# Edge products of 64 rows in the two halves of TensorE, four steps at a time in two banks

## The chip, the cores and the metric

The kernel runs on one core of a Trainium2 chip. The metric is the device time of one execution in microseconds; before and after are compared by the medians of several runs. The profile is that of one execution, taken by the hardware profiler.

## What is computed

Two graph layers with layer norm and residual on 6250 nodes of 256 features and 100000 edges. Every layer takes, for every node, the maximum over its incoming edges. The edges come sorted by `dst`.

```
def layer0(x, src, dst):                       # sweep 0
    e = relu((x[dst] - x[src]) @ theta_w.T + theta_b + x[src] @ phi_w.T + phi_b)
    return segment_max(e, dst)                 # 0 for a node without edges
x = layernorm(x + layer0(x, src, dst))
hv = x @ W_in + b_in
for W, b in ((W_u0, b_u0), (W_u1, b_u1)):      # sweeps 1 and 2
    m = relu(concat([hv[src], he]) @ W + b)    # he: 64 features per edge
    hv = where(has_in, segment_max(m, dst) + hv, hv)
out = layernorm(x + relu(hv @ W_ro + b_ro))
```

In sweeps 1 and 2 the product of `he` (64 features) with the last 64 rows of `W` is made per edge; the rest, `hv @ W[:256]`, is made per node and gathered. These are the edge products of the title.

## The kernel before

The edges are laid out as 782 steps of 128 edges, in 14 blocks (56 steps each, the last 54): partition p holds consecutive edges of a block along its steps. A sweep (`sweep(r)`, r = 0, 1, 2) walks the steps s = 0 to 781. Everything is in the order in which it is written (a manual schedule): every engine has its own queue, executes it in that order, and waits on semaphores.

**Gathers.** `sources(s)` (L790) is one indirect DMA on GpSimd (POOL): 128 rows of `table[r]` into step s of a tile `run` of 8 steps; there are 4 such tiles. It is issued 16 steps ahead (`AHEAD`). Sweeps 1 and 2 issue their first 24 steps (`EARLY`) from the end of the sweep before, with clipped indices that leave out node tile 0, whose table rows come last; these 24 steps get the rows of tile 0 by a one-hot product. Sweep 0 makes the first two steps of its first 20 tiles from raw rows of `x` instead (`raw_turn` transposes four blocks on TensorE, L798, ScalarE copies them, L800, `raw_pair` multiplies, L806).

**Edge products.** `pair(i)` serves two steps 2i and 2i+1. The features of both lie one above the other in `hT` (rows 0 to 63 the first step, rows 64 to 127 the second), and `whe` is a block-diagonal matrix of 128 rows by 512 columns, half of it zero. One product (L825) gives both steps in one bank of PSUM (`hp`, tag `he`, 3 banks). `pair` is issued 4 steps ahead. For the first 12 pairs SyncE fetches a row of indices (`row`, L822), VectorE makes a one-hot from it (`own`, L824), and two more products (L829) add the rows of node tile 0. `row` and `own` have two buffers each.

**The chain on VectorE.** For every two steps, L1030 adds the gathered rows of both to the bank `hp`; then each step does L1043, `run[s] = max(min(run[s-1], lim), row)`, a running maximum along the steps, which starts anew where the node changes.

**What follows.** When a tile of 8 steps is done, SyncE writes it to DRAM (`S<-run`, L1051); the buffer is free for new gathers when that has landed. At a block's end, `over_lanes` transposes the last step (`lp`, tag `tp`), `scan` on VectorE carries the maximum across the lanes, `back` transposes it back (`cp`, tag `tp`). Per tile of 128 nodes, `node` gathers the ends from S (L870, POOL), joins them with the carried ones and makes the node's products and the next table (`turned` with tag `tp`, `times` with tag `pr`). These are tasks, put into a list per step by `at(slot, f)` and called at the end of that step in the order in which they were put in. Sweep 0 also counts edges per node with one-hots (`count`: `ol` L710, `hist` L721).

**PSUM** has 8 banks: 3 of tag `he`, 2 of `tp`, 2 of `pr`, 1 of `v`.

Of the kernel before, what the change touches and what calls it, by code (L numbers as in the profile page):

```python
# [8 lines left out]
F32 = mybir.dt.float32  # L9
BF16 = mybir.dt.bfloat16  # L10
I32 = mybir.dt.int32
AF = mybir.ActivationFunctionType
OP = mybir.AluOpType
# [4 lines left out]
P = 128  # L18
N = 6250
D = 256  # L20
DE = 64
E = 100000
NT = 49
K = 8
# [11 lines left out]
BLOCKS = [56] * 13 + [54]  # L36
NB = len(BLOCKS)
FS = sum(BLOCKS)
FE = P * FS
FIRST = [sum(BLOCKS[:b]) for b in range(NB)]  # L40
# [4 lines left out]
EARLY = 3 * K  # L45
RAW = 40
# [21 lines left out]
def raw(s):  # L68

    i = s // K * 2 + s % K  # L70
    return i if s % K < 2 and i < RAW else None
# [525 lines left out]
def in_order(ctx: ExitStack, tc: tile.TileContext, g):  # L597
# [8 lines left out]
    nc = tc.nc  # L606
# [3 lines left out]
    s_e, head, x, x_sb, wd, s_r = (g[n] for n in ("s_e", "head", "x", "x_sb", "wd", "s_r"))  # L610
    part = g["part"]
    ctx.enter_context(tc.manual_schedule())
    one = ctx.enter_context(tc.tile_pool(name="one", bufs=1))
    work = ctx.enter_context(tc.tile_pool(name="work", bufs=2))
    psum = ctx.enter_context(tc.tile_pool(name="psum", bufs=2, space=PSUM))
# [9 lines left out]
    new0 = one.tile([P, D], F32, name="new0")  # L625
# [26 lines left out]
    bro = line(g["b_ro"], "bro")  # L652
    whe = []
    for r, w in enumerate((g["w_u0"], g["w_u1"])):
        t = one.tile([P, 2, D], F32, name=f"whe{r}")
        nc.vector.memset(t, 0.0)
        for s in range(2):
            nc.scalar.dma_start(t[s * DE:(s + 1) * DE, s, :], w[D:, :])
        whe.append(t)


# [38 lines left out]
    half = (NG + 1) // 2  # L700
    low = []
    for i in range(2):
        low.append(psum.tile([P, 512], F32, tag="he", name="low", bufs=3))
        n = min(half * K, FS - i * half * K)
        nc.scalar.copy(low[i][:, :n], lo[:, i * half * K:i * half * K + n])

# [18 lines left out]
    sums = []  # L725
# [29 lines left out]
        nc.vector.tensor_scalar(dest, a, mv[:, 0:1], sd, OP.subtract, OP.mult)  # L755

    def turned(a):
        tp = psum.tile([P, 512], F32, tag="tp", name="tp")
        for k in range(2):
            nc.tensor.transpose(tp[:, k * P:(k + 1) * P], a[:, k * P:(k + 1) * P], ident)  # L760
        aT = work.tile([P, 2, P], F32, name="aT")
        nc.scalar.copy(aT.rearrange("p k e -> p (k e)"), tp[:, :2 * P])  # L762
        return aT

    def times(aT, w, n, tag="pr"):
        ps = psum.tile([P, 512], F32, tag=tag, name="prod", bufs=3 if tag == "he" else 2)
        for k in range(2):
            nc.tensor.matmul(ps[:, :n], aT[:, k, :], w[:, k, :], start=(k == 0), stop=(k == 1))  # L768
        return ps

    def sweep(r):

        tasks = {}

        def at(slot, f, *a):
            tasks.setdefault(slot, []).append((f, a))
# [5 lines left out]
        runs = ahead.pop(r, {})  # L782
# [10 lines left out]

        def raw_turn(i):

            tp = psum.tile([P, 512], F32, tag="tp", name="tp")
            for q in range(4):
                nc.tensor.transpose(tp[:, q * P:(q + 1) * P], x_sb[:, 2 * i + q // 2, q % 2 * P:(q % 2 + 1) * P], ident)  # L798
            rT[i] = work.tile([P, K // 2, P], F32, tag="hT", name="rT", bufs=4)
            nc.scalar.copy(rT[i].rearrange("p k e -> p (k e)"), tp)  # L800

        def raw_pair(i):
            aT = rT.pop(i)
            hp[i * K // 2] = psum.tile([P, 512], F32, tag="pr", name="hp")
            for q in range(4):
                nc.tensor.matmul(hp[i * K // 2][:, q // 2 * D:(q // 2 + 1) * D], aT[:, q, :], wd[:, q % 2, :],  # L806
                                 start=q % 2 == 0, stop=q % 2 == 1)
# [5 lines left out]
            hT[c] = work.tile([P, K // 2, P], F32, name="hT", bufs=4)  # L813
            nc.scalar.dma_start(hT[c].rearrange("p q e -> p (q e)"), heT[c])

        def pair(i):
            c, q = divmod(i, K // 2)
            hp[i] = psum.tile([P, 512], F32, tag="he", name="hp", bufs=3)
            early = 2 * i < EARLY
            if early:  # L820
                row = work.tile([P, 2 * P], I32, name="row")
                nc.sync.dma_start(row, head[i:i + 1, :].to_broadcast([P, 2 * P]))  # L822
                own = work.tile([P, 2 * P], F32, name="own")
                nc.vector.tensor_scalar(own, row, part, None, OP.is_equal)  # L824
            nc.tensor.matmul(hp[i], hT[c][:, q, :], whe[r - 1].rearrange("p s f -> p (s f)"), start=True,  # L825
                             stop=not early)
            if early:
                for k in range(2):
                    nc.tensor.matmul(hp[i][:, k * D:(k + 1) * D], own[:, k * P:(k + 1) * P], new0, start=False, stop=k == 1)  # L829
            if q == K // 2 - 1:  # L830
                del hT[c]

        def over_lanes(b, last):

            lp = psum.tile([P, 512], F32, tag="tp", name="lp")
            nc.tensor.transpose(lp[:, 2 * P:3 * P], link[:, b:b + 1].to_broadcast([P, P]), ident)
            lim2 = work.tile([P, P], F32, name="lim2")
            nc.scalar.copy(lim2, lp[:, 2 * P:3 * P])
            for k in range(2):
                nc.tensor.transpose(lp[:, k * P:(k + 1) * P], last[:, k * P:(k + 1) * P], ident)  # L840
            to, of = cT[b % 2], cT[(b + 1) % 2]

            def scan():
                for k in range(2):
                    nc.vector.tensor_tensor_scan(to[:, k, 1:], lim2, lp[:, k * P:(k + 1) * P],
                                                 of[:, k, P:] if b else 0.0, OP.min, OP.max)
                if b:
                    nc.scalar.copy(to[:, :, 0:1], of[:, :, P:])
                else:
                    nc.vector.memset(to[:, :, 0:1], 0.0)  # L850

            def back():
                cp = psum.tile([P, 512], F32, tag="tp", name="cp")
                for k in range(2):
                    nc.tensor.transpose(cp[:, k * P:(k + 1) * P], to[:, k, :P], ident)
                carried_in.append(b)
                nc.scalar.copy(cs[:, b % KEPT, :D], cp[:, :D])

            at(FIRST[b] + BLOCKS[b], scan)
            at(FIRST[b] + BLOCKS[b] + 1, back)  # L860

        def node(t, g, b):

# [129 lines left out]
        b = 0  # L993
        for t in reversed(range(NT)):
            e = max(FIRST[SPAN[t][1]] + BLOCKS[SPAN[t][1]], begin)
            b = max(b + (gap if b < FS else 3), e + 4, min(e + AHEAD + 4, FS + 4))
# [11 lines left out]
        for s in range(-AHEAD if r == 0 else 0, FS):  # L1008
            if s + AHEAD < FS and (r == 0 or s + AHEAD >= EARLY):
                sources(s + AHEAD)  # L1010
            if r < 2 and s >= FS - FIRM:
                sources_next(s - (FS - FIRM))
            if s < 0:
                continue
            c, j = divmod(s, K)
            if r > 0:
                if s == 0:
                    for i in range(4):
                        features(i)
                    pair(0)  # L1020
                    pair(1)
                elif j == 0 and c + 3 < NG:
                    features(c + 3)
            if s % 2 == 0:
                two = runs[c][:, j:j + 2, :].rearrange("p s f -> p (s f)")
                if r > 0:
                    if s + 4 < FS:
                        pair(s // 2 + 2)
                    sums = hp.pop(s // 2)
                    nc.vector.tensor_add(sums, sums, two)  # L1030
                elif raw(s) is not None:
                    sums = hp.pop(s // 2)
                    i = raw(s) // 2
                    if i + 2 < RAW // 2:
                        raw_turn(i + 2)
                    if i + 1 < RAW // 2:
                        raw_pair(i + 1)
                else:
                    sums = two
            cur = runs[c][:, j, :]  # L1040
            row = sums[:, s % 2 * D:(s % 2 + 1) * D]
            if s > FIRST[blk]:
                nc.vector.scalar_tensor_tensor(cur, prev, lim[:, s:s + 1], row, OP.min, OP.max)  # L1043
            elif r > 0 or raw(s) is not None:
                nc.vector.tensor_copy(cur, row)
            prev = cur
            if j == K - 1 or s in (FS - 3, FS - 1):
                k = 2 if s == FS - 1 else j + 1
                to = S_w[P * FIRST[blk]:P * (FIRST[blk] + BLOCKS[blk]), :].rearrange("(p s) f -> p s f", p=P)
                at_ = s + 1 - k - FIRST[blk]  # L1050
                pending.append(nc.sync.dma_start(to[:, at_:at_ + k, :], runs[c][:, j + 1 - k:j + 1, :]))  # L1051
            if s == FIRST[blk] + BLOCKS[blk] - 1:
                over_lanes(blk, prev)
                blk += 1
            for f, a in tasks.pop(s, ()):
                f(*a)
# [62 lines left out]
```

## Time and profile before

| | |
|---|---|
| median of 7 runs | 3215.57 us (3211.86 to 3218.49) |
| profiled execution | 3214.67 us, span 3212.9 us |
| busy share of the span | PE 59%, DVE 66%, ACT 7%, POOL 75% |
| mean granted TensorE clock | 0.738 |
| first gather (L790) of sweep 0, 1, 2 | 61.8 us, 1091.6 us, 2143.4 us |

The profile names lines of the kernel (L825), engines (PE is TensorE, PEld its weight loads, DVE VectorE, ACT ScalarE, POOL GpSimd, SP SyncE) and tiles by their names in the program. A TensorE product of this type is recorded as two instructions.

### The profile page before, as it was taken

How to read it: one execution, taken by the hardware profiler on the slowest of the kernel's cores; microseconds unless marked ns; L12 is line 12 of the kernel's file. 1: busy time of each engine (PE TensorE's matmuls, PEld its weight loads, DVE VectorE, ACT ScalarE, POOL GpSimd, SP SyncE). 2: the span in 40 equal slices, each digit the busy share in tenths (PEclk: the TensorE clock that was granted, in tenths of full speed). 3: DMA queues.
4: the chain of work that ended last, by engine and by line, in shares of the span. 5: the costliest groups of instructions: out<-in, count | busy, mean ns of one | idle time of the engine just before them, and what ended most of it. 6: DMA issues, size and time to landing. Idle time of an engine off the chain costs nothing. (4 is left out here: it accounts for less than half of the span.)

```text
span 3212.9 us, 21650 instructions
## 1 busy us (share of the span) xinstructions
PE 1879.6 (59%) x4631; PEld 848.0 (26%) x4631; DVE 2127.8 (66%) x4750; ACT 238.7 (7%) x618; POOL 2394.8 (75%) x2500
## 2 busy tenths in 40 slices
PE   6663336566511266766666666657666666666665
PEld 5442222222200122322222222223332232222222
DVE  2788756555544376666666666657777777777766
ACT  2000001111100000000000000000001000000000
POOL 6767777777777767777777777776777777777775
PEclk8765557655655598788777877779888878887787
DMA  8769666656666676677767776767766676677775
GB/s 305 239 220 317 222 216 211 207 193 205 205 203 206 201 248 231 229 234 236 232 228 241 239 237 229 241 217 248 240 231 229 230 238 228 233 234 241 238 232 192
DMA packets 241821, 739.39 MB, mean 230 GB/s; under 512 B 52485, under 2 KB 95858, under 8 KB 204434
## 3 DMA queue, kind: packets, MB, share of 16 engines
q0 software_dynamic: 119664, 326.92, 34.2%
q1 hardware_dynamic: 69568, 337.85, 28.1%
q10 hardware_dynamic: 52450, 73.16, 6.9%
q8 instruction: 39, 0.64, 0.1%
q14 instruction: 100, 0.82, 0.1%
HBM read 404.56 MB, written 333.17 MB: 230 GB/s over the span
## 5 line engine op out<-in xcount | busy, mean ns | idle before, releaser
L790 POOL DMA_INDIRECT run<-table,s_s x2258 | 2165.6, 959 | 718.0 <-issue 606.2
L825 PE MATMUL hp<-whe,hT 128*128 128x512 f32 x1564 | 1055.2, 784 | 530.0 <-DVE run L1043 515.1
L1030 DVE TENSOR_TENSOR hp<-hp,run 128x512 f32<-128x512 f32 x782 | 543.9, 695 | 459.1 <-DMA run<-table,s_s 422.3
L1043 DVE SCALAR_TENSOR_TENSOR run<-run,lim,hp 128x256 f32<-128x256 f32 x1573 | 753.9, 479 | 46.8
L825 PEld LDWEIGHTS hp<-whe,hT 128*128 128x128 f32 x1564 | 326.5, 239 | 1077.0 <-DVE run L1043 1016.7
L1043 DVE SCALAR_TENSOR_TENSOR run<-run,lim 128x256 f32<-128x256 f32 x731 | 351.6, 481 | 233.3 <-DMA run<-table,s_s 220.7
L889 PE MATMUL v<-cs,pick 128*128 128x256 f32 (+1 forms) x438 | 167.4, 503 | 141.6 <-DVE pick L882 137.0
L768 PE MATMUL prod<-wcat,aT 128*128 128x512 f32 x196 | 174.4, 1041 | 23.2 <-ACT aT L762 23.2
L870 POOL DMA_INDIRECT m<-S,end_i x147 | 144.1, 981 | 52.6 <-issue 43.6
L889 PEld LDWEIGHTS v<-cs,pick 128*128 128x128 f32 x438 | 105.2, 260 | 253.9 <-issue 150.0
L721 PE MATMUL hist<-oh,ol 128*128 128x8 bf16 (+7 forms) x782 | 34.8, 167 | 177.7 <-DVE oh L716 177.7
L710 DVE TENSOR_TENSOR ol<-col,low 128x1024 bf16<-128x1024 bf16 x98 | 118.7, 1212 | 7.3 <-PE hist L721 7.3
L760 PE MATMUL tp<-ident,h_sb 128*128 128x128 f32 x196 | 49.1, 339 | 121.7 <-DVE h_sb L935 121.3
L932 ACT ACTIVATE m<-m,has 128x256 f32<-128x256 f32 x98 | 49.7, 508 | 692.4 <-DVE m L931 690.9
L760 PE MATMUL tp<-ident,x_sb 128*128 128x128 f32 x98 | 31.9, 426 | 113.6 <-DVE x_sb L755 85.7
L840 PE MATMUL lp<-ident,run 128*128 128x128 f32 x84 | 24.2, 383 | 124.1 <-DVE run L1043 116.4
L768 PE MATMUL prod<-wro,aT 128*128 128x256 f32 x196 | 79.1, 542 | 25.3 <-ACT aT L762 25.3
L721 PEld LDWEIGHTS <-ol 128*128 128x128 bf16 x782 | 36.3, 104 | 203.0 <-DVE ol L710 198.4
L768 PE MATMUL prod<-wt,xT 128*128 128x256 f32 x196 | 88.0, 596 | 0.4 <-DMA xT<-in_xTn 0.4
L762 ACT COPY aT<-tp 128x256 f32<-128x256 f32 x147 | 54.7, 372 | 449.4 <-PE tp L760 427.4
L768 PEld LDWEIGHTS prod<-wcat,aT 128*128 128x128 f32 x196 | 56.1, 314 | 89.1 <-issue 48.4
L760 PEld LDWEIGHTS tp<-ident,h_sb 128*128 128x128 f32 x196 | 23.9, 164 | 210.8 <-issue 122.5
(131 smaller groups left out, 1323.6 us busy)
## 6 DMA issues: line engine op xcount, KB each, us to landing
S<-run SPq DMA_DIRECT2D x291, 1024.0 KB, 4.8
hT<-in_heT ACTq DMA_DIRECT2D x196, 256.0 KB, 4.5
run<-table,s_s POOLq DMA_INDIRECT x2258, 3.4
table<-new ACTq DMA_DIRECT2D x98, 128.0 KB, 3.6
xg<-in_xTn SPq DMA_DIRECT2D x7, 896.0 KB, 9.5
xT<-in_xTn SPq DMA_DIRECT2D x49, 128.0 KB, 5.1
x_sb<-in_xn SPq DMA_DIRECT2D x7, 896.0 KB, 7.7
out<-new ACTq DMA_DIRECT2D x48, 128.0 KB, 2.5
```

Of the source, the lines that this page charges most:

```text
L710: nc.vector.tensor_tensor(ol[:, :k, :], col.unsqueeze(1).to_broadcast([P, k, P]), low[c // half][:, c % half * K:c % half * K + k].unsquee ...
L721: nc.tensor.matmul(hist[:, t0:t0 + w], ol[:, j, :], oh[:, j, :w], start=False, stop=(c == NG - 1 and j == k - 1))
L760: nc.tensor.transpose(tp[:, k * P:(k + 1) * P], a[:, k * P:(k + 1) * P], ident)
L762: nc.scalar.copy(aT.rearrange("p k e -> p (k e)"), tp[:, :2 * P])
L768: nc.tensor.matmul(ps[:, :n], aT[:, k, :], w[:, k, :], start=(k == 0), stop=(k == 1))
L790: nc.gpsimd.indirect_dma_start(out=runs[s // K][:, s % K, :], out_offset=None, in_=table[r][:SPARE + 1, :] if early else table[r], in_offs ...
L825: nc.tensor.matmul(hp[i], hT[c][:, q, :], whe[r - 1].rearrange("p s f -> p (s f)"), start=True, stop=not early)
L870: i = nc.gpsimd.indirect_dma_start(out=o["m"], out_offset=None, in_=S_r[:P * (FIRST[SPAN[t][1]] + BLOCKS[SPAN[t][1]]), :], in_offset=bass. ...
L889: nc.tensor.matmul(o["v"][:, :N1], p, cs[:, blk % KEPT, :N1], start=(blk == SPAN[t][0]), stop=(blk == SPAN[t][1]))
L932: nc.scalar.activation(o["m"], o["m"], AF.Relu, scale=has[:, t:t + 1])
L1030: nc.vector.tensor_add(sums, sums, two)
L1043: nc.vector.scalar_tensor_tensor(cur, prev, lim[:, s:s + 1], row, OP.min, OP.max)
```

## The change

`whe` becomes one matrix of 64 rows by 256 columns, held twice, in partitions 0 to 63 and in partitions 64 to 127; its two fills with zero go. `pair(i)` becomes `four(u)`, which serves steps 4u to 4u+3 in two banks. The first steps of the two pairs (4u, 4u+2) come out of rows 0 to 63 and go to the first bank, the second steps (4u+1, 4u+3) come out of rows 64 to 127 and go to the second. It is issued when step 4u-4 begins. VectorE adds the gathered rows of steps 4u and 4u+2 in one instruction at step 4u, and those of 4u+1 and 4u+3 at step 4u+1. The running maximum stays one instruction per step. In the first 24 steps the two one-hots of a four are made ahead of its products.

Tag `he` gets 4 banks, and tag `tp` 1 in place of 2. `scan` and `back` are put at the front of their step's task list.

```diff
     for r, w in enumerate((g["w_u0"], g["w_u1"])):
-        t = one.tile([P, 2, D], F32, name=f"whe{r}")
-        nc.vector.memset(t, 0.0)
+        t = one.tile([P, D], F32, name=f"whe{r}")
         for s in range(2):
-            nc.scalar.dma_start(t[s * DE:(s + 1) * DE, s, :], w[D:, :])
+            nc.scalar.dma_start(t[s * DE:(s + 1) * DE, :], w[D:, :])
...
-        tp = psum.tile([P, 512], F32, tag="tp", name="tp")
+        tp = psum.tile([P, 512], F32, tag="tp", name="tp", bufs=1)
...
-        ps = psum.tile([P, 512], F32, tag=tag, name="prod", bufs=3 if tag == "he" else 2)
+        ps = psum.tile([P, 512], F32, tag=tag, name="prod", bufs=4 if tag == "he" else 2)
...
-        def pair(i):
-            c, q = divmod(i, K // 2)
-            hp[i] = psum.tile([P, 512], F32, tag="he", name="hp", bufs=3)
-            early = 2 * i < EARLY
-            if early:
-                row = work.tile([P, 2 * P], I32, name="row")
-                nc.sync.dma_start(row, head[i:i + 1, :].to_broadcast([P, 2 * P]))
-                own = work.tile([P, 2 * P], F32, name="own")
-                nc.vector.tensor_scalar(own, row, part, None, OP.is_equal)
-            nc.tensor.matmul(hp[i], hT[c][:, q, :], whe[r - 1].rearrange("p s f -> p (s f)"), start=True,
-                             stop=not early)
-            if early:
+        def four(u):
+
+            c, q = divmod(u, K // 4)
+            hp[u] = [psum.tile([P, 512], F32, tag="he", name="hp", bufs=4) for _ in range(2)]
+            early = 4 * u < EARLY
+            n = min(2, FS // 2 - 2 * u)
+            for j in range(n):
+                i = 2 * u + j
+                if early:
+                    row = work.tile([P, 2 * P], I32, name="row")
+                    nc.sync.dma_start(row, head[i:i + 1, :].to_broadcast([P, 2 * P]))
+                    own = work.tile([P, 2 * P], F32, name="own")
+                    nc.vector.tensor_scalar(own, row, part, None, OP.is_equal)
                 for k in range(2):
-                    nc.tensor.matmul(hp[i][:, k * D:(k + 1) * D], own[:, k * P:(k + 1) * P], new0, start=False, stop=k == 1)
-            if q == K // 2 - 1:
+                    at_ = slice(k * DE, (k + 1) * DE)
+                    nc.tensor.matmul(hp[u][k][:, j * D:(j + 1) * D], hT[c][at_, 2 * q + j, :], whe[r - 1][at_, :],
+                                     start=True, stop=not early)
+                if early:
+                    for k in range(2):
+                        nc.tensor.matmul(hp[u][k][:, j * D:(j + 1) * D], own[:, k * P:(k + 1) * P], new0, start=False,
+                                         stop=True)
+            if q == K // 4 - 1:
                 del hT[c]
...
-            at(FIRST[b] + BLOCKS[b], scan)
-            at(FIRST[b] + BLOCKS[b] + 1, back)
+            for i, f in enumerate((scan, back)):
+                tasks.setdefault(FIRST[b] + BLOCKS[b] + i, []).insert(0, (f, ()))
...
-                    pair(0)
-                    pair(1)
+                    four(0)
...
-                if r > 0:
-                    if s + 4 < FS:
-                        pair(s // 2 + 2)
-                    sums = hp.pop(s // 2)
-                    nc.vector.tensor_add(sums, sums, two)
...
+            if r > 0:
+                if s % 4 == 0 and s + 4 < FS:
+                    four(s // 4 + 1)
+                if s % 4 < 2:
+                    n = min(2, (FS - s + 1) // 2)
+                    sums = hp[s // 4][s % 2].rearrange("p (a f) -> p a f", f=D)[:, :n, :]
+                    nc.vector.tensor_add(sums, sums, runs[c][:, j:j + 2 * n - 1:2, :])
+                row = hp[s // 4][s % 2][:, s % 4 // 2 * D:(s % 4 // 2 + 1) * D]
+                if s % 4 == 3:
+                    del hp[s // 4]
```

## The prediction, made before the changed kernel was run

> **What bounds the kernel now.** First the busy times and the waits of POOL: is an engine full, and what does it wait for?
>
> ```profile
> PE 1879.6 (59%) x4631; PEld 848.0 (26%) x4631; DVE 2127.8 (66%) x4750; ACT 238.7 (7%) x618; POOL 2394.8 (75%) x2500
> POOL run L790 <- issue: 620.2, 2032, 1.2
> POOL run L790 <- DVE run L1043: 43.6, 58, 7.5
> POOL m L870 <- issue: 43.6, 143, 0.3
> ```
>
> No engine looks full, but POOL is: a gather takes 0.95 us, and 0.30 us pass before the next with nothing awaited ("issue"), one per 1.25 us. The 2493 of L790, L870 and L76 at that pace are 3116 of the span's 3212.9 us. So what the end depends on is POOL's standing still beyond 0.30 us. I listed every such gap: 9.3 us in the prologue, 10.5 us in sweep 0 between 155 and 226 us (seven gaps), 11.8 us at the start of sweep 1, 7.8 us at that of sweep 2, 7.8 us before the last row gather. Nowhere else in 3000 us. The timeline of POOL, start of sweep 1:
>
> ```profile
> 1140.11 0.94 POOL L790 DMA_INDIRECT run<-table,s_s  x1 [7.45 <-DVE run L1043]
> 1141.35 0.95 POOL L790 DMA_INDIRECT run<-table,s_s  x1 [0.30 <-issue]
> ...
> 1153.93 0.95 POOL L790 DMA_INDIRECT run<-table,s_s  x1 [4.13 <-DVE run L1043]
> ...
> 1164.78 0.94 POOL L790 DMA_INDIRECT run<-table,s_s  x1 [1.15 <-DVE run L1043]
> ```
>
> There are four run tiles; POOL waits until VectorE has finished a tile and its `S<-run` has landed. After 1165 us VectorE is ahead for good: S of tile 2 leaves at 1159.39 us (step 23 done), and that moment alone fixes how late POOL is for the rest of the sweep. What VectorE does until then, from the timeline of all engines:
>
> ```profile
> 1119.99 2.08 PE L825 MATMUL hp<-whe,hT 128*128 128x512 f32 x2 [6.87 <-DMA hT<-in_heT]
> 1123.81 0.35 DVE L824 TENSOR_SCALAR own<-row,part 128x256 f32<-128x256 int32 x1 [9.54 <-PE hp L829]
> 1124.08 0.69 DVE L1030 TENSOR_TENSOR hp<-hp,run 128x512 f32<-128x512 f32 x1
> ...
> 1126.28 0.35 DVE L824 TENSOR_SCALAR own<-row,part 128x256 f32<-128x256 int32 x1 [0.53 <-PE hp L829]
> ...
> 1138.36 0.35 DVE L824 TENSOR_SCALAR own<-row,part 128x256 f32<-128x256 int32 x1 [6.28 <-DMA row<-in_head]
> ```
>
> Last the edge products, in the groups of instructions:
>
> ```profile
> L825 PE MATMUL hp<-whe,hT 128*128 128x512 f32 x1564 | 1055.2, 784 | 530.0 <-DVE run L1043 515.1
> L1030 DVE TENSOR_TENSOR hp<-hp,run 128x512 f32<-128x512 f32 x782 | 543.9, 695 | 459.1 <-DMA run<-table,s_s 422.3
> ```
>
> PE waits for VectorE, VectorE for gathers. Cheaper products gain nothing along the sweeps.
>
> **The change part by part.**
>
> *Products along the sweeps: 0.* Two pairs had 2 x 512 columns, a four has 4 x 256: the same columns if the halves run one after another, half if both run at once. L825 falls from 1055 us to between 530 and 1100 us. POOL's gathers hide it (gaps 0.30 us from 1165 to 2184 and 2213 to 3193 us). Cover gone: see the second rival. The Trainium skill (TensorEngine Tiling (Array Packing), section "Key Properties") says that such tiles load weights and multiply independently of each other, but also, against this change, that going from one tiling mode to another drains TensorE; nothing in this trace shows either, as all its products have the full height. By the first the sum below would stand at its low end, by the second at its high end.
>
> *VectorE along the sweeps: 0.* L1030 becomes 784 instructions of the same 512 elements (0.69 us). Step 4u now awaits gather 4u+2 in place of 4u+1, and after gather 4u+3 one add and three L1043 remain (0.69 + 3 x 0.51 = 2.2 us) in place of an add and two (1.7 us). It is 0.5 us later; a tile must be free only 24 gathers (30 us) after its last one was issued, of which landing (3.4), VectorE and S (5) take some 12. The two fills with zero (1.02 us at 51.6 us) stood where VectorE idled: 0.
>
> *Start of sweeps 1 and 2.* VectorE's queue now has `own` 0 to 3 ahead of the first add, not 0 to 2. `own` has two buffers, so `own` 3 waits until PE has read `own` 1. That moment is in the trace: 1126.28. The first add moves from 1124.08 to 1126.55; then add, copy, add and three L1043 (0.73 + 0.46 + 0.73 + 3 x 0.51 = 3.45, start to start in this stretch) end steps 0 to 3 at 1130.0, and steps 4 to 7 take 2 x 1.91 (before's pace per pair): 1133.8 against 1132.1. That is +1.7 us if the halves run one after another. At once, the two cold edge products (1.87 and 1.64 us) fall towards half, and nothing is left: 0. I take 1.2. Then `row` 6 and 7, on SyncE's queue behind `S<-run`, which waits for step 7: both are now needed before the add, and the second is issued 0.48 us after the first (1133.00, 1132.52): +0.3. `own` 9 needs the products with `own` 7, which ended 4.9 us after `own` 6 began (1143.3 - 1138.4), where VectorE is there after 4.6: +0 to 0.5. The third stage (`row` 10, 11) has the same +0.3, and its fours wait for PE instead: 0 to 0.7. Sum per sweep 0.6 to 3.5, I take 2.5, nearer to one after another, as the products of an early four alternate with full-height ones. Twice: **+5.0** (1.2 to 7.0). Each such us delays step 23, S, POOL and the end one to one.
>
> *One `tp` bank in sweep 0.* The start, from the timeline:
>
> ```profile
> 69.29 1.06 ACT L800 COPY rT<-tp 128x512 f32<-128x512 f32 x2
> 69.92 3.78 PE L806 MATMUL hp<-wd,rT 128*128 128x256 f32 x8 [14.24 <-ACT rT L800]
> ...
> 73.74 0.42 DVE L1045 COPY run<-hp 128x256 f32<-128x256 f32 x1 [20.97 <-PE hp L806]
> ```
>
> The second turn (four transposes, 0.6 to 1.1 us) was done long before; with one bank it follows the first copy and stands ahead of the first product: +0.9 (0.6 to 1.1). From there to 226 us VectorE never waits for a gather but for PE and back, and POOL waits for VectorE, so all of it arrives. At the ends of blocks 0 and 1, `lp` holds the bank until `scan`, and the next turn (130.29 before) waits for that (131.0): +0.7, and +0.6 at the second; PE's `hist` behind it holds VectorE's `ol` (idle 0.86 us there already). Bounds: 0 and 1.9 for both. Sum **+2.2** (0.6 to 3.0). Moving `scan` and `back` forward only changes places within a step: 0. The fourth `he` bank: 0, as `prod` in it is read a step later and made once in eight.
>
> *The tail.*
>
> ```profile
> 3194.86 0.70 DVE L1030 TENSOR_TENSOR hp<-hp,run 128x512 f32<-128x512 f32 x1 [3.21 <-DMA run<-table,s_s]
> ```
>
> From here before does two adds and four L1043: 3.4 us. After, gather 779 finds step 776 done at best: add, three L1043, then steps 780 and 781 with adds of 256 elements (0.42): 0.73 + 1.53 + 2 x 0.46 + 2 x 0.51 = 4.2. **+0.8** (-0.5 if gather 780 comes late, 2.0 if step 776 waits too). S, the last row gather and its chain follow one to one.
>
> Sum 5.0 + 2.2 + 0.8 = 8.0 (1.3 to 12.0). The profiled execution took 3214.67 us (span 3212.9 and 1.8 around it), 0.9 below the median of 3215.57. So 3222.7 by the profile and 3223.6 by the median; I say 3223. About 0.2% (6.4 us) is what a measurement can tell from no change.
>
> **Rivals.**
>
> *The halves run at once and the starts cost little: same.* For it: the two products of a pair of steps lie next to each other in PE's queue, in different rows and banks. Then the starts give 1 us, the sum is 1 to 6, and the time 3216 to 3221.
>
> *PE becomes the pace: far slower.* From 1170 to 2160 us PE is busy 642 of 990 us, 507 of them L825. If 64-row products took twice as long per column (loads not hidden, drains), PE would need 1149 us: 160 us more per sweep, some 3530 us. It decides from 855 us of edge products per sweep, 1.7 times now. Milder drains, at the 0.24 us that PE's loads sit idle for "issue" here, four in each of six early fours, add at most 5.8 us per sweep.
>
> *Faster: POOL's standing at the starts shrinks.* PE is what VectorE waits for from 1119.99 to 1123.81 us and 0.53 us later: 4.3 us per sweep. If the split products cut that nearly whole, and `tp` and tail cost nothing, it is -8.6 us: 3206. It decides if `own` 3 begins before 1123.8 us; half-cost edge products alone, 0.93 + 1.71 (`own` 0) + 0.8 + 0.86 (`own` 1) after 1119.99, reach only 1124.3. That speaks against it.
>
> **Chances.** My forecast, +6.4 to +20: 0.62. Far slower: 0.04. Same: 0.27. Faster: 0.07. So slower 0.66. The range goes from 3213 (the sum's low end less the 3.7 us by which runs scatter below the median) to 3235 (3215.6 + 12.0 + half the drains of both sweeps, and scatter).
>
> **What would show it.** POOL's page row unchanged at 2395 us, gaps of 0.30 us along the sweeps; the gaps at the starts of sweeps 1 and 2 adding up to 14 and 10 us instead of 11.8 and 7.8, those between 155 and 226 us to 13; first add after `own` 3. Wrong if POOL stands still in the middle of a sweep, if those sums fall, or if the edge products pass 1700 us.

## The result and the profile after

The changed kernel takes 3225.27 us (median of 15 runs, 3219.88 to 3227.57) beside 3215.14 us of the kernel before (35 runs on the same chip): 1.0029 times as long, 95% interval 1.0023 to 1.0036. It is slower, by 10.1 us of the medians. A second set of the two gave 3225.03 (8 runs) and 3215.12 us, 1.0028 [1.0018, 1.0039].

The profiled execution took 3238.39 us (span 3236.6), 13 us above the median of its runs. That of the second set took 3224.81 (span 3222.8) and is the typical one. I show the first where a single stretch is read, and the second where times are added up. First the busy times, the waits of POOL and the two costliest groups, in the first profile after:

```profile
PE 1812.9 (56%) x6195; PEld 1093.7 (34%) x6195; DVE 2128.9 (66%) x4750; ACT 238.8 (7%) x618; POOL 2398.2 (74%) x2500
```

```profile
POOL run L789 <- issue: 617.9, 2019, 2.1
POOL run L789 <- DVE run L1053: 64.7, 93, 8.6
```

```profile
L830 PE MATMUL hp<-whe,hT 64*128 64x256 f32 x3128 | 860.7, 613 | 423.6 <-DVE run L1053 409.8
L1035 DVE TENSOR_TENSOR hp<-hp,run 128x512 f32<-128x512 f32 (+1 forms) x784 | 543.7, 693 | 475.8 <-DMA run<-table,s_s 399.7
```

POOL's own work and its "issue" row are as before; its wait for VectorE's L1053 (L1043 before) has grown from 43.6 to 64.7 us (57.0 in the second profile). The edge products (L830, L825 before) have become 195 us cheaper, and the kernel slower: PE had been waiting, and waits longer now. The timeline of POOL at the start of sweep 1, in the second profile, where before it stood 7.45, 4.13 and 1.15 us:

```profile
1141.46 0.95 POOL L789 DMA_INDIRECT run<-table,s_s  x1 [8.19 <-DVE run L1053]
...
1157.42 0.95 POOL L789 DMA_INDIRECT run<-table,s_s  x1 [6.20 <-DVE run L1053]
...
1168.36 0.94 POOL L789 DMA_INDIRECT run<-table,s_s  x1 [1.22 <-DVE run L1053]
```

Nearly all that was lost here lies in the first two of the three stops. What POOL stands still beyond its pace of one gather in 1.25 us, summed by place, with what single gathers take over 0.946 us ("stretch"), in us:

| kernel | span | prologue | sweep 0 | start of sweep 1 | start of sweep 2 | before the last row gather | stretch |
|---|---|---|---|---|---|---|---|
| before | 3212.9 | 9.3 | 10.5 | 11.8 | 7.8 | 7.8 | 35.7 |
| after, first profile | 3236.6 | 8.8 | 22.1 | 15.5 | 11.3 | 8.0 | 39.2 |
| after, second profile | 3222.8 | 7.5 | 10.5 | 14.7 | 12.3 | 6.9 | 40.3 |

Each span less its row's other terms leaves 3130 to 3132 us, so the account leaves out nothing of size: POOL stands still nowhere else. The two starts have 7.2 and 7.4 us more than before, most of the 10.1. The 13 us of the first profile come mainly from sweep 0, which varies so much in the same kernel that the medians of many runs must decide on it.

### The profile page after: what moved, and what is told of

It reads as the page before. It is cut to its first block, busy times and chain, and to the rows that moved or that the text cites. A ratio compares the mean times of both kernels' runs of the same rounds, so it can differ in the third digit from the quotient of the medians.

```text
span 3236.6 us, 24789 instructions
## 1 busy us (share of the span) xinstructions
PE 1812.9 (56%) x6195; PEld 1093.7 (34%) x6195; DVE 2128.9 (66%) x4750; ACT 238.8 (7%) x618; POOL 2398.2 (74%) x2500
## 5 line engine op out<-in xcount | busy, mean ns | idle before, releaser
L830 PE MATMUL hp<-whe,hT 64*128 64x256 f32 x3128 | 860.7, 613 | 423.6 <-DVE run L1053 409.8
L1035 DVE TENSOR_TENSOR hp<-hp,run 128x512 f32<-128x512 f32 (+1 forms) x784 | 543.7, 693 | 475.8 <-DMA run<-table,s_s 399.7
L830 PEld LDWEIGHTS hp<-whe,hT 64*128 64x128 f32 x3128 | 543.1, 293 | 719.2 <-DVE run L1053 566.2
L1053 DVE SCALAR_TENSOR_TENSOR run<-run,lim,hp 128x256 f32<-128x256 f32 x1573 | 754.3, 480 | 47.0
L1053 DVE SCALAR_TENSOR_TENSOR run<-run,lim 128x256 f32<-128x256 f32 x731 | 351.8, 481 | 221.0 <-DMA run<-table,s_s 207.0
L895 PE MATMUL v<-cs,pick 128*128 128x256 f32 (+1 forms) x438 | 200.9, 588 | 178.4 <-DVE pick L888 178.4
L895 PEld LDWEIGHTS v<-cs,pick 128*128 128x128 f32 x438 | 111.7, 287 | 281.7 <-DVE pick L888 139.1
L759 PE MATMUL tp<-ident,h_sb 128*128 128x128 f32 x196 | 56.7, 385 | 214.9 <-DVE h_sb L941 214.9
L709 DVE TENSOR_TENSOR ol<-col,low 128x1024 bf16<-128x1024 bf16 x98 | 118.7, 1212 | 10.4 <-PE hist L720 10.3
L767 PE MATMUL prod<-wro,aT 128*128 128x256 f32 x196 | 96.0, 642 | 25.6 <-ACT aT L761 25.6
L767 PE MATMUL prod<-wu,aT 128*128 128x256 f32 x196 | 80.9, 556 | 8.3 <-ACT aT L761 7.5
```

The costliest lines, as they stand in the source:

```text
L709: nc.vector.tensor_tensor(ol[:, :k, :], col.unsqueeze(1).to_broadcast([P, k, P]), low[c // half][:, c % half * K:c % half * K + k].unsquee ...
L830: nc.tensor.matmul(hp[u][k][:, j * D:(j + 1) * D], hT[c][at_, 2 * q + j, :], whe[r - 1][at_, :], start=True, stop=not early)
L895: nc.tensor.matmul(o["v"][:, :N1], p, cs[:, blk % KEPT, :N1], start=(blk == SPAN[t][0]), stop=(blk == SPAN[t][1]))
L1035: nc.vector.tensor_add(sums, sums, runs[c][:, j:j + 2 * n - 1:2, :])
```

## The experiments

The theory: VectorE's queue has all `own` of a four ahead of its first add, and `own` has two buffers, so the starts of sweeps 1 and 2 wait for PE; one `tp` bank adds a little in sweep 0. Rivals: the half products themselves (drains, a lower clock), or the single bank as the main cause. Every ratio is against runs of the kernel before on the same chip.

**The changed kernel again.** `after_again` repeats it, for a second profile.

> The changed kernel once more, for a second profile. Theory (three places): the 10 us lie in POOL's standing beyond 0.30 us, some 15.5 us at the start of sweep 1 (before 11.8) and 11.3 at that of sweep 2 (before 7.8), as in the first profile; the 22 us of the first profile in sweep 0 (before 10.5) are mostly chance of that execution and fall to 12 to 14. Time 3225, ratio 1.003. Rival (sweep 0 is the main cost): the standing in sweep 0 stays near 22 us.

Measured: 1.0028, as above. The loss is there with sweep 0 at 10.5 us, so the outlier of the first profile isn't its cause.

**The bank alone.** `before_tp1` is the kernel before with one `tp` bank and the earlier `scan` and `back`:

```diff
-        tp = psum.tile([P, 512], F32, tag="tp", name="tp")
+        tp = psum.tile([P, 512], F32, tag="tp", name="tp", bufs=1)
...
-            at(FIRST[b] + BLOCKS[b], scan)
-            at(FIRST[b] + BLOCKS[b] + 1, back)
+            for i, f in enumerate((scan, back)):
+                tasks.setdefault(FIRST[b] + BLOCKS[b] + i, []).insert(0, (f, ()))
```

> The kernel before with one bank for tag tp and with scan and back at the front of their lists, nothing else. Theory: sweep 0 alone changes, its standing between 100 and 240 us grows by 2.2 us (0.6 to 3.0), the starts of sweeps 1 and 2 stay at 11.8 and 7.8; time 3217.4 (3215.8 to 3218.2). Rival (the bank is hidden, all 10 us come from the edge products): 3215.1. Rival (the bank is the main cost): 3222 and more.

> The kernel before with one tp bank once more, since what is left of the change outside the two starts, some 3 to 4 us, has no proven place. Theory (it is the bank): ratio 1.0007 (1.0002 to 1.0010), standing in sweep 0 above 12 us. Rival (the bank costs nothing, as the first time): ratio 0.9995 to 1.0005, and the 10 to 22 us of standing in sweep 0 are chance.

Measured: 3213.92 us (11 runs), 0.9999 [0.9990, 1.0008], and, run a second time, 3221.09 us (11), 1.0005 [0.9996, 1.0014]. No cost can be told from zero, and over 4.5 us is excluded. The bank isn't the main cause. Its profiles have 17.3 and 12.5 us of standing in sweep 0, and 11.3 and 6.4, then 11.9 and 5.9 us at the starts, where 11.8 and 7.8 had been expected to stay. Why the start of sweep 2 is up to 2 us shorter here, no run shows.

**Full-height edge products in the new order.** `after_full` keeps the fours, the banks and the order of the one-hots, but multiplies all 128 rows, half of them by zeros:

```diff
-                    at_ = slice(k * DE, (k + 1) * DE)
-                    nc.tensor.matmul(hp[u][k][:, j * D:(j + 1) * D], hT[c][at_, 2 * q + j, :], whe[r - 1][at_, :],
+                    nc.tensor.matmul(hp[u][k][:, j * D:(j + 1) * D], hT[c][:, 2 * q + j, :], whe[r - 1][:, k, :],
```

> The changed kernel with edge products of 128 rows by 256 columns (half the weights zero again), one for each step: order, banks and one-hots as in the changed kernel, but no halves and no change of height. Theory (the starts cost more because two one-hots stand in VectorE's queue ahead of the first add of a four and wait for PE): the standing stays near 15.5 and 11.3 us or grows by up to 1 us each as the halves no longer overlap, time 3225 to 3227, edge products back to 1050 to 1150 us and the granted clock to 0.74. Rival (changes of height drain TensorE, or the lower clock makes the starts slow): the standing falls to about 12 and 8 us, time 3218.

Measured: 3223.89 us (9 runs), 1.0026 [1.0016, 1.0036]; starts 14.1 and 13.0 us. The loss stays with no half product in the kernel. The edge products from 1180 to 2160 us, by windows of time (length, PE busy with the records, weight loads busy, granted clock, DMA share, GB/s), of before, of after and of this kernel:

```profile
1180.00:2160.00 980.00, 500.01 (x729) 155.25 (x728) 0.80 0.71 235
```

```profile
1180.00:2160.00 980.00, 402.10 (x1489) 260.79 (x1485) 0.60 0.71 236
```

```profile
1180.00:2160.00 980.00, 463.02 (x1466) 339.65 (x1465) 0.81 0.71 235
```

The clock falls to 0.60 with the half products alone, and the loss is the same at 0.81. So the clock along the sweeps isn't its cause either.

**The new order in the old kernel.** `before_hots` has the old products and pairs, but makes the one-hots of two pairs together:

```diff
+        def hots(u):
+            for i in range(2 * u, min(2 * u + 2, EARLY // 2)):
+                row = work.tile([P, 2 * P], I32, name="row")
+                nc.sync.dma_start(row, head[i:i + 1, :].to_broadcast([P, 2 * P]))
+                owns[i] = work.tile([P, 2 * P], F32, name="own")
+                nc.vector.tensor_scalar(owns[i], row, part, None, OP.is_equal)
...
+                    if s % 4 == 0:
+                        hots(s // 4 + 1)
```

> The kernel before, its products and adds unchanged, but the one-hots of the first 24 steps made two at a time as in the changed kernel. Theory A (the queue order of the one-hots with two buffers is the cost): the standing grows to about 14 to 15 and 10 to 12 us as in the changed kernel, time 3221 to 3223. Theory B (the cost is that an add over two pairs needs the products of both): the standing stays at 11.8 and 7.8, time 3215. Both can bind by themselves, since own 3 waits for the same product as the first add of a four does: then the standing grows here too, and the next run tells.

Measured: 3227.30 us (5 runs) against 3218.20, 1.0036 [1.0022, 1.0050]; starts 15.7 and 13.0 us, 9.1 more than in before, and the medians differ by 9.1 (6 to 8 were expected). Its profiled execution, 3219.97 us, is the fastest of the five. The order of these one-hots (with the loads of their rows), and nothing else of the change, makes the whole loss. Its VectorE at the start of sweep 1:

```profile
1120.87 0.35 DVE L821 TENSOR_SCALAR own<-row,part 128x256 f32<-128x256 int32 x1 [1.59 <-PE hp L833]
1121.13 0.69 DVE L1037 TENSOR_TENSOR hp<-hp,run 128x512 f32<-128x512 f32 x1
...
1140.41 0.35 DVE L821 TENSOR_SCALAR own<-row,part 128x256 f32<-128x256 int32 x1 [1.45 <-PE hp L833]
```

The first add stands behind `own` 3, and `own` 3 behind PE. Later the same happens to `own` 9.

**The old order in the new kernel.** `after_early_pairs` runs steps 0 to 23 in pairs with full-height products, and fours of halves from step 24 (the early part of `four` goes; `pair` of before is back, with its bank among the four of `he`):

```diff
+                if s % 2 == 0 and s + 4 < EARLY:
+                    pair(s // 2 + 2)
-                if s % 4 == 0 and s + 4 < FS:
+                if s % 4 == 0 and EARLY <= s + 4 < FS:
                     four(s // 4 + 1)
```

> The changed kernel, but steps 0 to 23 of sweeps 1 and 2 made as before: pairs of 128 rows in one bank, one-hots one pair at a time, adds of two neighbouring steps. Fours in halves from step 24 on. Theory (the whole cost lies in these 24 steps): the standing goes back to 11.8 and 7.8 us at the two starts, the clock stays near 0.6; time 3215 to 3219, ratio 1.000 to 1.001. Rival (the fours along the sweeps, the low clock or the single bank also cost): 3222 and more, ratio above 1.002.

Measured: 3221.10 us (11 runs), 1.0014 [1.0004, 1.0023]; starts 11.8 and 8.3 us, before's to within half a microsecond. The timeline of POOL:

```profile
1142.75 0.94 POOL L790 DMA_INDIRECT run<-table,s_s  x1 [7.05 <-DVE run L1065]
...
1156.59 0.94 POOL L790 DMA_INDIRECT run<-table,s_s  x1 [4.15 <-DVE run L1065]
...
1167.83 0.94 POOL L790 DMA_INDIRECT run<-table,s_s  x1 [1.54 <-DVE run L1065]
```

The starts are repaired, half products along the sweeps notwithstanding. What is left, 2.9 us of the medians and above the 1.001 expected, isn't there. Over all profiles the two starts together are 17.7 to 20.1 us with the old order of these steps (before, the two `before_tp1`, and `after_early_pairs` and `after_pairs_he`) and 26.6 to 28.7 with the new one (the two of after, `after_full`, `before_hots`, `after_turn_he`).

**The turn's bank.** `after_turn_he` takes the bank of sweep 0's turns from the four of `he`, and `after_pairs_he` joins that with the early pairs:

```diff
-            tp = psum.tile([P, 512], F32, tag="tp", name="tp", bufs=1)
+            tp = psum.tile([P, 512], F32, tag="he", name="tp", bufs=4)
```

> The changed kernel with the transposes of the raw rows in sweep 0 in banks of tag he (four) in place of the single tp bank. Theory: the first product of sweep 0 no longer waits for a second turn, nor the turns at the ends of blocks for scan: the standing in sweep 0 falls by 2.2 us (0.6 to 3.0), time 3223 (3222 to 3224.6), sweeps 1 and 2 unchanged. Rival (the bank is hidden): 3225.

> Early steps in pairs as before, and the raw transposes of sweep 0 in the he banks: both named costs undone, the fours in halves from step 24 on remain. Theory: nothing is left, ratio 1.0000 (0.9993 to 1.0008), standing 10 to 12, 11.8 and 8 us. Rival (the halves along the sweeps, at the lower clock, cost something by themselves): ratio 1.0014 as with the pairs alone.

Measured: 3222.37 us (11 runs), 1.0023 [1.0014, 1.0032], and 3218.85 us (11), 0.9998 [0.9989, 1.0007]. With both repairs the change is worth nothing and costs nothing. How much the bank contributes stays open: by the ratios it is 0.0005 without the early pairs (1.0028 - 1.0023) and 0.0016 with them (1.0014 - 0.9998), 2 and 5 us, beside some 0.0013 by which such a difference is uncertain; the two `before_tp1` say about 1 us (their medians are 1.2 below and 2.6 above).

**More buffers.** `after_own4` gives `own` four buffers instead of two:

```diff
-                    own = work.tile([P, 2 * P], F32, name="own")
+                    own = work.tile([P, 2 * P], F32, name="own", bufs=4)
```

> The changed kernel with four buffers for the one-hots in place of two: VectorE no longer waits for TensorE before making one. Theory A (queue order): the standing falls by 2 us and more at each start, to 12 and 8.5 us, time 3219. Theory B (the adds need both products of a four anyway): the first add comes at most 0.5 us earlier, the standing falls by 0 to 1.5 us per start, time 3222 to 3225.

> Four one-hot buffers once more: the profile showed 2 us less standing at each start, the times showed no gain. Theory: ratio 1.0016 to 1.0020 (4 us below the changed kernel), standing 13.5 and 9.5. Rival: ratio 1.0028 as the changed kernel.

Measured: 3226.11 us (6 runs), 1.0031 [1.0018, 1.0044], and 3224.46 (11), 1.0016 [1.0006, 1.0027]: the time is inconclusive. The starts are clearer, 13.5 and 9.4 us, 13.6 and 9.1 the second time: 4 us less than in after, of the 7. What the rest waits for:

```profile
1122.15 0.70 DVE L1035 TENSOR_TENSOR hp<-hp,run 128x512 f32<-128x512 f32 x1 [3.63 <-PE hp L834]
```

No `own` stands in front of PE any more, and the first add waits for PE itself: a bank of a four holds columns of both pairs, so that its add needs the `own` products of both. Buffers repair one of two causes.

**The rows earlier.** `after_early_rows` keeps all of the change but asks for each `row` one four earlier, with four buffers, so that the loads no longer stand behind `S<-run` on SyncE's queue:

```diff
+        def fetch(u):
+            for i in range(2 * u, min(2 * u + 2, EARLY // 2)):
+                ids[i] = work.tile([P, 2 * P], I32, name="row", bufs=4)
+                nc.sync.dma_start(ids[i], head[i:i + 1, :].to_broadcast([P, 2 * P]))
...
+            if u == 0:
+                fetch(0)
+            fetch(u + 1)
```

> The changed kernel with four buffers for the rows of indices, each fetched one four earlier, so that rows 6, 7 and 10, 11 stand ahead of the write of S in SyncE's queue. Theory (POOL's standing at the starts is VectorE's lateness at step 23, and two waits of 5.5 to 6.3 us for these rows are the largest part of it): the standing at each start falls by 8 to 12 us, to about 3 to 6 and 1 to 3 us; time 3205 (3202 to 3212), below the kernel before. Rival (the landing of S or the gathers set the standing, and the row waits are covered): 3220 to 3225.

Measured: 3213.12 us (11 runs), 0.9987 [0.9978, 0.9997]; starts 6.4 and 5.1 us. POOL, start of sweep 1:

```profile
1142.16 0.94 POOL L789 DMA_INDIRECT run<-table,s_s  x1 [6.25 <-DMA S<-run]
...
1152.59 0.94 POOL L789 DMA_INDIRECT run<-table,s_s  x1 [0.74 <-DVE run L1060]
```

The second stop falls from 6.2 to 0.74 us and the third is gone. The gain of 5 us by the medians is smaller than the 10 expected, and 5.1 us are left at the start of sweep 2, where 1 to 3 were expected. The 15.5 us saved at the starts, against the second profile of after, show as 13 us by the two ratios (1.0028 - 0.9987).

**A better version.** `after_best` has the early rows and the turn's bank in `he`, and in the first 24 steps issues the second pair of a four two steps after the first, as before's order had it:

```diff
-                    four(s // 4 + 1)
+                    four(s // 4 + 1, (0,) if s + 4 < EARLY else (0, 1))
+                if s % 4 == 2 and s + 4 < EARLY:
+                    four(s // 4 + 1, (1,))
```

> The changed kernel with rows fetched one four earlier (four buffers), the raw transposes in the he banks, and in the first 24 steps the one-hot and products of a four's second pair two steps later. Theory: standing at the starts 6.4 and 5.1 us or up to 3 us less each, sweep 0 at 10 to 12, time 3205 to 3212, ratio 0.997 to 0.999, faster than the kernel before and than the changed one. Rival (with the rows early, the order of the one-hots no longer binds, and sweep 0 is chance): 3213, ratio 0.9987.

Measured: 3207.95 us (6 runs) against 3218.47, 0.9965 [0.9952, 0.9977]; starts 5.0 and 3.2 us. It is faster than both kernels, first of all by the earlier rows (0.9987 alone). No run has them in the kernel before, and `after_pairs_he` (0.9998) gives no gain that could be credited to the half products.

## Why the prediction was right, point by point

**The bound and the mechanism were right.** POOL's busy row stayed (2398 for 2395 us), its gaps along the sweeps stayed at 0.30 us, and what VectorE loses at the starts reaches the end one to one. The order of the one-hots was named as the cause, and `before_hots` and `after_early_pairs` show it from both sides.

**Starts of sweeps 1 and 2: +5.0 forecast, 7.2 and 7.4 measured, a term that was too small.** Per sweep that is 3.6 to 3.7, just above the upper bound of 3.5. VectorE and PE in the first profile after:

```profile
1129.12 1.22 PE L830 MATMUL hp<-whe,hT 64*128 64x256 f32 x4 [6.48 <-DMA hT<-in_heT]
1132.38 0.38 DVE L827 TENSOR_SCALAR own<-row,part 128x256 f32<-128x256 int32 x1 [8.65 <-PE hp L834]
...
1135.20 0.35 DVE L827 TENSOR_SCALAR own<-row,part 128x256 f32<-128x256 int32 x1 [2.44 <-PE hp L834]
1135.47 0.69 DVE L1035 TENSOR_TENSOR hp<-hp,run 128x512 f32<-128x512 f32 x1
...
1148.62 0.76 DVE L827 TENSOR_SCALAR own<-row,part 128x256 f32<-128x256 int32 x2 [5.57 <-DMA row<-in_head]
...
1154.30 0.35 DVE L827 TENSOR_SCALAR own<-row,part 128x256 f32<-128x256 int32 x1 [1.21 <-PE hp L834]
```

Counted from the landing of `hT` (the first of these rows; 1119.99 before), the step on `own` 3 held: the first add comes 6.35 us later, 4.09 before, so +2.26 where the sum had 2.47. S of tile 0 leaves 13.95 us after `hT` for 12.12, +1.83 where I took 1.2. My 0 for halves that run at once was wrong as a bound: they do, and 1.83 is still lost, since `own` 3 waits for the full-height `own` products (L834), and these run at a granted clock of 0.59 from 1129 to 1136 us. The wait for the next `row` (up to `own` 6 and `own` 10) shrank by 0.7 and then grew by 0.2, where no change was taken; the +0.3 taken each time was for the second `row`, and VectorE waits for it 0.34 us at `own` 11, while at `own` 7 the profile shows no wait. From `own` 6 to S of tile 1 it is 9.34 us for 7.73: +1.61, where the wait of `own` 9 was given 0 to 0.5. This is the largest miss. `own` 9 begins 5.68 us after `own` 6 (1154.30 - 1148.62), not the 4.6 to 4.9 that before's products gave. What it waited for is in the timeline of PE, first before, then after:

```profile
1142.28 1.03 PE L829 MATMUL hp<-new,own 128*128 128x256 f32 x4
```

```profile
1152.19 2.07 PE L834 MATMUL hp<-new,own 128*128 128x256 f32 x4
```

These are the products with `own` 7, which `own` 9 waits for. Before, PE had come to full clock by then; after, it had not (0.50 from 1148.6 to 1154.3 us). The prediction had taken the pace of PE here from one execution of before. The half products aren't the reason: in `before_hots`, where all products have the full height, the clock is 0.50 from 1134.9 to 1139.8 us and `own` 9 waits 1.45 us (its line is shown above). In the four starts of `after_full` and `before_hots`, without a half product, it is 12.9 to 14.1 us from `hT` to S of tile 0 and 8.95 to 9.60 from `own` 6 to S of tile 1; in the four of after it is 12.9 to 14.0 and 9.34. So the order makes both terms. The last stage has +0.96, where 0.3 to 1.0 was given with its second `row`. Sum 1.83 - 0.70 + 1.61 + 0.23 + 0.96 = 3.93 us.

**Products along the sweeps: 0, right, and the rival that halves run at once was half right.** They do, where the clock is full. PE after step 23, in the first profile after:

```profile
1169.37 1.14 PE L830 MATMUL hp<-whe,hT 64*128 64x256 f32 x8
...
1178.53 2.59 PE L830 MATMUL hp<-whe,hT 64*128 64x256 f32 x8 [0.70 <-DVE run L1053]
```

Eight records are the four products of a four: 1.14 us, where full-height products of the same 1024 columns take 2.08 in `after_full`, and one of 512 columns alone took 1.02 to 1.13 in before. Three fours later they take 2.59. The cheap starts that this rival also needed did not come, since the starts wait for the `own` products, which the halves don't shorten.

The Trainium skill (TensorEngine Tiling (Array Packing), "Key Properties") says that a change of tiling mode drains TensorE, and gives no size. Here the weight load stands idle 0.33 us for "issue" at the change of height before the 1.14 us row, beside 0.24 between before's full-height products. That is a tenth of a microsecond, and with no height changed at all (`before_hots`) the loss was the same. The rule didn't decide this case. That such tiles run independently of each other, which the page also says, agrees with the 1.14 us.

**Tail: +0.8 forecast, none measured.** VectorE's last chain did grow, from 3.4 to 4.0 us (3216.83 to 3220.8 in the first profile), but POOL's stop before the last row gather was 8.0 and 6.9 us after, 7.8 before: within what the same kernel scatters.

**Sweep 0: +2.2 forecast, consistent but not settled.** At the start, VectorE's first copy comes 5.20 us after ACT's first (70.24 to 75.44), 4.45 before: +0.75 for 0.9. The ends of the blocks can't be read from single profiles. Where the turns have one bank, nine profiles have 10.5 to 22.1 us of standing in sweep 0, mean 15.1; where the bank isn't shared so, five have 10.3 to 17.2, mean 12.6. That is 2.5 us, less than the scatter, and by the timed runs the bank is worth somewhere between nothing and 5 us.

**The other rivals.** PE as the pace: no, its edge products fell to 861 us, and past their starts POOL does not stop in sweeps 1 and 2 until the last row gather. Faster: this would have needed `own` 3 within 3.8 us of `hT`; it came after 6.08. The forecast's 8.0 us for 10.1 is thus 5.0 for 7.3 at the starts, 0.8 for about 0 at the tail, and 2.2 for the unsettled rest. That the total came so near is in part luck, since these misses have opposite signs.

## What to carry to other kernels

Ask of a change first whether its engine is waited for. Here 195 us of PE's work bought nothing, and the few microseconds at the start of each sweep were most of the loss: there, grouping work in fours put one-hots that wait for PE ahead of an add that had not waited for them, and what the products cost moved that by tenths of a microsecond. When work is grouped, keep what only the first part needs ahead of what the last part waits for, and count the buffers: with four in place of two no one-hot waited for PE any more, but a second cause (the bank shared by both pairs) was still there. And look at what stands behind a write in a DMA queue: loads moved ahead of it gave back more than the change had cost.

## What was not expected of the hardware

**Less work brought a lower clock.** The mean granted clock fell from 0.738 to 0.599 over the kernel and from 0.80 to 0.60 along sweep 1, and was 0.81 with full-height products in the same order. At full clock four half products take 1.14 us, along the sweep 2.2 in the mean (402.10 us for 1489 records, 8 to a four), so a good part of the saving went back: L830 is 861 us where 1055 would have halved to some 530. After step 23, while VectorE catches up, a four comes every 3.28 us. In `after_full` its products last 2.08 us of these, and the granted clock is 1.00 from 1161 to 1205 us:

```profile
1166.11 2.08 PE L830 MATMUL hp<-whe,hT 128*128 128x256 f32 x8 [1.20 <-DVE run L1053]
```

In after they last 1.14 us at first, at a granted clock of 1.00 (1169 to 1175.6 us), and later 2.59, at 0.50 (1176 to 1230 us). Between them:

```profile
1171.96 1.65 PE L830 MATMUL hp<-whe,hT 64*128 64x256 f32 x8 [1.46 <-DVE run L1053]
1175.25 2.58 PE L830 MATMUL hp<-whe,hT 64*128 64x256 f32 x8 [1.64 <-DVE run L1053]
```

The Trainium skill (TensorE: Matmul & The Clock Gate, "HAM oscillation — how this bites in real kernels") describes a loop whose bursts are shorter than the DMA waits between them, where such a wait crosses a window of more than 3.4 us and the next burst starts at half clock. The trace agrees that short bursts lose the clock, but not on the length of the wait: between 1165 us and the fall PE never waited longer than 1.64 us.

**Single profiles scatter by more than the change.** Standing in sweep 0 was 22.1 and 10.5 us in two executions of one kernel, and the stretch of the gathers was 32.6 and 41.1 us in two of another (`after_own4`).
